# A two-layer graph network in Strassen products: four tasks in the first group, new step orders at the layer change and in layer 1, and a last transition matrix made transposed

## Chip, cores and metric

The kernel runs on one core of a Trainium2 chip. The metric is the device time of that core in microseconds, the median of three runs.

## The reference

128 graphs of 128 nodes with 512 features go through two layers; `x` is 128x128x512 and `adj` 128x128x128.

```python
# layer 0
deg = jnp.sum(adj, axis=-1, keepdims=True)
agg = jnp.einsum('bij,bjf->bif', adj, x) / jnp.maximum(deg, EPS)
out = jnp.einsum('bnf,of->bno', jnp.concatenate([x, agg], axis=2), W)
x = _layernorm(x + jax.nn.relu(out), axis=-1)
# layer 1
e = jax.nn.leaky_relu(sj[:, None, :] + si[:, :, None] + ab[0], negative_slope=0.2)
alpha_matrix = A * jnp.exp(e)
transition = alpha_matrix / (jnp.sum(alpha_matrix, axis=-1, keepdims=True) + 1e-12)
for k in range(Wk.shape[0]):
    H = H + Xk @ Wk[k] + bk[k]
    Xk = jnp.einsum('bij,bjd->bid', transition, Xk)
x = _layernorm(x + jax.nn.relu(H), axis=-1)
```

`sj` and `si` are two linear functions of a node's features, through `Wv` and `aw`; the kernel folds them into two more columns of the big product.

## The kernel before

**Groups and tasks.** The graphs go in 32 groups of four through layer 0, then through layer 1. The products with the weights use a two-level scheme with seven products in the place of eight at each level. An outer product is a *task*, its seven inner products are *steps* (written O5.3: task O5, step 3; inner products in the order 1, 5, 6, 2, 7, 3, 4). A step of layer 0 is two records of 256 columns, one of layer 1 two of 385 (all matmuls come from `mm`, line 149). The left operands of the products are node blocks, transposed on DVE (`x_turn`, L254), and their sums: `x_inner` (L242 to L245) for the inner level, `x_s1` to `x_s4` (L265 to L277) for the outer level, all on POOL. The weights' sums are `w_inner` (L931 to L934) and `w_outer` (L939).

**Lanes.** Tasks run in two lanes of four PSUM banks each, `bA` for lane 0 and `bB` for lane 1. In a task, ACT copies the bank of step 1 (L617) and that of step 2 (L623, into `s`), DVE adds step 3 (L626), the banks of steps 4 and 6 are evicted, the bank of step 5 is read by DVE (L650, L663) and by POOL (L660), that of step 7 late. So a step often has to wait for what ACT or DVE makes of an earlier step of its lane.

**Layer 0.** Group 0 runs one task F, an ordinary 2x2 product of blocks (14 steps of four matmuls), and FL, the product with the adjacency matrices. The other groups run P12, P56, P74 and T (their evictions at L309 to L321 and L355 to L357; `last`, L388, and `residual`, L371). `fold_constants` (L160 to L184) makes the folded columns and the biases; `degree`, `a_norm`, `a_load` and `a_turn` prepare the adjacency matrices.

**Layer 1.** A group runs O1, O2, O5, O6, O7, O4, O3 and C, the two products with the transition matrix. C and O3.7 lag one group and are then written in lower case (c.5, o3.7); x.1 to x.8 is the last C. `sum_r` (L696) and `sum_c` (L704) prepare the sums that C reads. The scores are taken out in `t_scores` (L712 to L723), turned into the transition matrix by `t_load`, `t_exp` (L743, L745), `t_sums` (L750 to L755) and `t_norm` (L762, L770), and transposed in `t_turn` (L777); in the last group `t_exp` and `t_norm` do it in place, with four PE transposes. Layer norm is `ln_mean`, `ln_var` (L493, squares on ACT), `ln_scales` and `ln_apply` (L506, on ACT); `y_store` and `load_y` (L95) keep and fetch the rows, and `load_left` fetches the node blocks.

**Order.** The order of the steps is written out by hand in strings: PA for a group of layer 0, PT for the layer change, PB for a group of layer 1, PL for the last. All else is put beside the steps by tables of positions: PLACES_A, PLACES_B, PLACES_M (last but one group), PLACES_L, PLACES_T (weight loads) and START. Position 2t comes after the instructions of step t, 2t + 1 after its late evictions. `need` checks that what an operation reads was issued before. Each engine's queue, SP's (which issues nearly all DMAs) and POOL's among them, is then taken in the order in which the code is written.

Of the kernel before, what the change touches and what calls it, by code (L numbers as in the profile page):

```python
# [1016 lines left out]
```

## Time and profile before

| | |
|---|---|
| median of three runs | 2112.71 us (2112.41 to 2116.83) |
| time of the profiled execution | 2111.64 us |
| its span | 2109.8 us, so 1.84 us lie outside it |
| granted clock of TensorE, mean | 0.997 |
| instructions | 25967 |
| busy: PE, DVE, ACT, POOL | 2083.5, 1464.6, 1145.5, 1539.4 us |
| PE busy from 0 to 60 us (start) | 53.22 us |
| 60 to 805 (layer 0) | 745.00 us |
| 805 to 864 (layer change) | 54.14 us |
| 864 to 2060 (layer 1) | 1193.61 us |
| 2060 to 2110 (end) | 37.48 us |

The last five rows are the busy time of PE in stretches of the span. PE counts as busy while a matmul is under way or held up inside a row of the timeline, so a short stall between two matmuls does not always show as idle time. In a row of the timeline the first number is the start, the second the length, then come the engine, the line, the destination and sources, the shape and the number of records; in brackets stand the idle time ahead of it and what ended that.

### The profile page before, as it was taken

To read this page: it belongs to the slowest core of one execution; us is meant where nothing else is said; L and a number is where in the kernel's file an instruction comes from. 1 tells how busy PE (TensorE), PEld (TensorE's weight loads), DVE (VectorE), ACT (ScalarE), POOL (GpSimd) and SP (SyncE) were. 2 spreads that over 40 slices of the span, in tenths; PEclk is the share of its full clock that TensorE was granted. 3 is DMA by queue.
4 is the path that set the end of the run, shared out by engine and by line. 5 is a ranking of instruction groups with operands and counts; after the bars stand their busy time and mean duration, and the time that the engine had idled before them with its cause. 6 is when DMAs were issued, how large, how long until landed. Compare 5 with 4: busy or idle time off the path is not lost.

```text
span 2109.8 us, 25967 instructions
## 1 busy us (share of the span) xinstructions
PE 2083.5 (99%) x7104; PEld 1328.1 (63%) x7104; DVE 1464.6 (69%) x3235; ACT 1145.5 (54%) x2879; POOL 1539.4 (73%) x1432
## 2 busy tenths in 40 slices
PE   8999999999999999999999999999999999999997
PEld 5887888888778886555555555555555555555553
DVE  4778777777777776666666666666666666666665
ACT  2665666666656665355455455455455455455454
POOL 5877888887767776767767767767767767767763
PEclk9999999999999999999999999999999999999999
DMA  7766666566566768334434434434434434434423
GB/s 177 183 186 190 189 184 173 159 190 192 160 173 182 191 164 239 76 91 121 109 91 119 112 91 121 109 91 120 111 91 120 111 91 120 111 91 121 110 71 115
DMA packets 429486, 287.13 MB, mean 136 GB/s; under 512 B 153497, under 2 KB 352281, under 8 KB 429340
## 3 DMA queue, kind: packets, MB, share of 16 engines
q1 hardware_dynamic: 428092, 283.62, 50.7%
q10 hardware_dynamic: 1120, 1.84, 0.4%
q8 instruction: 56, 0.92, 0.2%
q14 instruction: 90, 0.74, 0.1%
q0 software_dynamic: 128, 0.01, 0.0%
HBM read 191.60 MB, written 93.79 MB: 135 GB/s over the span
## 4 chain that ended last, share of the span: by engine, by line
PE 95%; DVE 2%; POOL 1%; DMA 1%; ACT 1%; issue 0%; ACTq 0%; SPq 0%; POOLq 0%; DVEq 0%
PE bB L149 50%; PE bA L149 45%; DVE y L371 1%; DVE r L663 1%; DMA xb<-in_x_dram 0%; DMA big<-wd 0%; DMA big<-in_w0t_dram 0%; PE bB L174 0%; POOL s L660 0%; ACT junk L493 0%; POOL r L696 0%; ACT T L762 0%; POOL xs L265 0%; POOL xs L269 0%; POOL xu L277 0%
## 5 line engine op out<-in xcount | busy, mean ns | idle before, releaser
L149 PE MATMUL bA<-big,xu 128*128 128x256 f32 (+1 forms) x1834 | 578.6, 435 | 3.3 <-DVE r L663 1.0
L149 PEld LDWEIGHTS bA<-big,xu 128*128 128x128 f32 x1834 | 345.6, 190 | 177.6 <-issue 25.7
L149 PE MATMUL bB<-big,xl 128*128 128x256 f32 (+1 forms) x1330 | 399.1, 416 | 0.2 <-ACT bB L617 0.2
L149 PE MATMUL bA<-big,xs 128*128 128x256 f32 (+1 forms) x1316 | 387.9, 418 | 0.2
L149 PEld LDWEIGHTS bB<-big,xl 128*128 128x128 f32 x1330 | 252.0, 190 | 99.3 <-issue 15.5
L149 PEld LDWEIGHTS bA<-big,xs 128*128 128x128 f32 x1316 | 245.1, 190 | 92.1 <-DVE bA L626 14.3
L149 PE MATMUL bB<-big,xu 128*128 128x256 f32 (+1 forms) x868 | 286.1, 440 | 2.6 <-DVE bB L388 2.5
L149 PE MATMUL bB<-c,TT 128*128 128x512 f32 x512 | 246.3, 594 | 0.0
L660 POOL TENSOR_TENSOR s<-s,r 128x385 f32<-128x385 f32 x128 | 127.6, 997 | 151.2 <-DVE bA L626 105.3
L493 ACT ACTIVATE junk<-y,mv 128x512 bf16<-128x512 f32 x252 | 181.6, 721 | 78.6 <-POOL mv L488 74.5
L149 PEld LDWEIGHTS bB<-big,xu 128*128 128x128 f32 x868 | 159.0, 189 | 91.7 <-DVE r L650 19.3
L506 ACT ACTIVATE y<-y,mv,rstd 128x512 f32<-128x512 f32 x252 | 201.4, 811 | 1.3 <-POOL mv L501 1.3
L626 DVE TENSOR_TENSOR bA<-bA,s 128x385 f32<-128x385 f32 x128 | 72.5, 567 | 165.6 <-ACT s L623 117.8
L149 PE MATMUL bA<-big,xl 128*128 128x385 f32 (+1 forms) x490 | 181.3, 476 | 4.2 <-DVE xl L254 4.1
L371 DVE SCALAR_TENSOR_TENSOR y<-bB,y 128x512 f32<-128x512 f32 x256 | 170.4, 682 | 19.8 <-PE bB L149 13.5
L149 PE MATMUL bB<-big,xs 128*128 128x385 f32 x448 | 173.5, 492 | 0.9 <-POOL xl L242 0.9
L149 PEld LDWEIGHTS bB<-c,TT 128*128 128x128 f32 x512 | 97.2, 190 | 89.4 <-issue 48.6
L797 ACT COPY bB<-r 128x512 f32<-128x512 f32 x64 | 37.7, 589 | 193.4 <-DVE big L796 188.2
L277 POOL TENSOR_TENSOR xu<-xu,xs 128x896 f32<-128x896 f32 x63 | 131.3, 2085 | 10.3 <-PE bA L149 10.3
L149 PEld LDWEIGHTS bA<-big,xl 128*128 128x128 f32 x490 | 93.3, 191 | 71.0 <-DVE c L663 7.9
L273 POOL TENSOR_TENSOR xl<-xu,xl 128x896 f32<-128x896 f32 x63 | 133.3, 2116 | 1.1
L269 POOL TENSOR_TENSOR xs<-xs,xu 128x896 f32<-128x896 f32 x63 | 131.7, 2090 | 2.4
(172 smaller groups left out, 3540.3 us busy)
## 6 DMA issues: line engine op xcount, KB each, us to landing
xb<-in_x_dram SPq DMA_DIRECT2D x256, 128.0 KB, 3.5
y<-in_x_dram SPq DMA_DIRECT2D x64, 512.0 KB, 4.5
yd<-y SPq DMA_DIRECT2D x64, 512.0 KB, 2.8
xb<-yd SPq DMA_DIRECT2D x256, 128.0 KB, 3.9
y<-yd SPq DMA_DIRECT2D x64, 512.0 KB, 4.4
out_dram<-y SPq DMA_DIRECT2D x62, 512.0 KB, 2.8
ag<-in_adj_dram SPq DMA_DIRECT2D x64, 256.0 KB, 4.0
sb<-sd SPq DMA_DIRECT2D x252, 64.0 KB, 3.1
```

The costliest lines, as they stand in the source:

```text
L149: nc.tensor.matmul(dst, lhsT, rhs, start=start, stop=True, skip_group_check=True)
L269: S_.tensor_sub(xs[n][:, 1], xs[n][:, 0], xu[n][:, 0])
L273: S_.tensor_sub(xl[n][:, 0], xu[n][:, 0], xl[n][:, 0])
L277: S_.tensor_sub(xu[n][:, 1], xu[n][:, 1], xs[n][:, 1])
L371: V.scalar_tensor_tensor(y, t, 0.0, y, ALU.max, ALU.add, accum_out=mvs[n][:, b, 0:1])
L493: L_.activation(junk, ys[n, b // 2][:, b % 2], AF.Square, bias=mvs[n][:, b, 0:1], accum_out=mvs[n][:, b, 1:2])
L506: L_.activation(y, y, AF.Identity, bias=mvs[n][:, b, 0:1], scale=rstds[n][:, b : b + 1])
L626: V.tensor_add(W, X, s5)
L660: S_.tensor_add(s5, s5, part(src, BZ, BW))
L663: V.tensor_add(part(dst, BZ, BW), X, s5)
L797: L_.copy(at_[b], row(b, 254, 766, 1))
```

## The change

**First group.** F becomes four tasks A to D of seven steps with two matmuls each: A and B are the first column of the weight blocks for the upper and lower node blocks, C and D the second. Each uses halves of the banks; C and D are evicted into banks of `bA`. The order is PF. The lanes are swapped (lane 0 now holds `bB`, lane 1 `bA`), and FL runs in `bA`. The inner sums of group 0 move from POOL to DVE, those of the lower blocks into START. Weight slots 1 and 3 are loaded by ACT and SP in turn instead of by ACT alone, `wvt` later on SP. The folding moves from beside F to beside group 1, into `bA`.

**Layer change and layer 1.** New strings PT, PB and PL, a string of its own (PG) for the first group of layer 1, and new positions throughout; PLACES_S gives the work around the layer change its own positions.

**Last group.** Its adjacency matrices come as blocks in four DMAs and are transposed on DVE (`adj_turn`). The matrix of scores is made transposed on PE (`end_scores`, ones times a diagonal of `si`, then Prelu with `sj` as bias, and Exp), multiplied by the transposed adjacency, and its sums over the partitions come from a matmul by ones, which gives them to all partitions (`end_rows`). `end_norm` adds the epsilon, takes the reciprocal and multiplies, in halves of two graphs, on DVE.

```diff
         g = n % NG
+        if n == 2 * NG - 1:
+            adjs[n] = p1.tile([P, G, Q, R], FP, name="agb", tag="ag")
+            load_blocks(adjs[n], adj[g * G : (g + 1) * G])
+            return
...
-    wvt_sb = [p2.tile([P, 2, F], FP, name=f"wvt{i}", tag="y") for i in range(2)]
+    wvt_sb = [p2.tile([P, 2, F], FP, name=f"wvt{i}", tag="c22") for i in range(2)]
...
-    load_w0([nc.scalar], 1)
-    load_w0([nc.scalar], 3)
+    load_w0([nc.scalar, nc.sync], 1)
+    load_w0([nc.scalar, nc.sync], 3)
...
+    def load_wvt():
+        for i in range(2):
+            nc.sync.dma_start(wvt_sb[i], wvt[i * FH : (i + 1) * FH, :].rearrange("(c p) f -> p c f", p=P))
...
-        pb, pc, pw = bB[0], bB[3], bB[0]
+        need(("FL", 0, 2))
+        pb, pc, pw = bA[2], bA[3], bA[2]
         nc.tensor.matmul(pb, ones_row[:K], bk_sb, start=True, stop=True)
...
-        left_sums([S_, S_, S_, S_], [t[:, :, i] for i in range(7)])
+        left_sums([S_ if n else V] * 4, [t[:, :, i] for i in range(7)])
...
+    def first(g, o, h):
+        X, Y, W, Z = [t[:, h * FH : (h + 1) * FH] for t in (bA, bB)[o]]
+        if o == 0:
+            dst = blocks(p2, "c21" if h else "c11")
+            (c21s if h else c11s)[g] = dst
+        else:
+            need(("w_inner", 1))
+
+        def prod(dst, k, start=False):
+            for i in range(2):
+                mm(dst, (xu, xl)[h][g][:, i, LEFT[k]], wf[:, SLOT[2 * i + o], RIGHT[k]], start and i == h == 0)
+
+        def evict(b, t):
+            if o == 0:
+                to = part(dst, b)
+            else:
+                need(("FA", 0, 7), ("FB", 0, 7))
+                to = bA[2 * h + b[0]][:, b[1] * FH : (b[1] + 1) * FH]
+            if (b[0] + b[1]) % 2:
+                L_.copy(to, t)
+            else:
+                V.tensor_copy(to, t)
+        s5 = halves()[:, :FH]
+        if h:
+            need(("F" + "AC"[o], 0, 2))
+        prod(X, 1, True)
+        L_.copy(Y, X)
+        yield
+        prod(Z, 5, True)
+        L_.copy(s5, Z)
+        yield
+        prod(X, 6)
+        V.tensor_add(W, X, s5)
+        yield
+        prod(Y, 2)
+        late.append((evict, BY, Y))
+        yield
+        prod(X, 7)
+        V.tensor_add(Z, X, s5)
+        yield
+        prod(W, 3)
+        late.append((evict, BWW, W))
+        yield
+        prod(X, 4)
+        late.append((evict, BZ, Z))
+        late.append((evict, BX, X))
+        yield
...
-                V.tensor_scalar(dg[:, b], ident, sj[:, b : b + 1], None, ALU.mult)
+                V.tensor_scalar(dg[:, b], ident, si[:, b : b + 1], None, ALU.mult)
...
+    def adj_turn():
+        need(("load_adj", 2 * NG - 1))
+        src = adjs[2 * NG - 1]
+        adjs[2 * NG - 1] = p1.tile([P, G, N], FP, name="agT", tag="aT")
+        V.transpose(adjs[2 * NG - 1].rearrange("p g n -> p (g n)"), src.rearrange("p g j r -> p (g j r)"))
+
+    def end_scores(g):
+        need(("t_scores", g), ("C", g - 1, 8))
+        (dg, _), pt = Ts[g], lanes[0][0]
+        mm(pt, ones[:].to_broadcast([P, P]), dg, True)
+        T = TTs[g] = p1.tile([P, G, N], FP, name="TT")
+        for b in range(G):
+            L_.activation(T[:, b], pt[:, b * N : (b + 1) * N], AF.Prelu, bias=sj[:, b : b + 1], alpha=SLOPE)
+            if b % 2:
+                L_.activation(T[:, b - 1 : b + 1], T[:, b - 1 : b + 1], AF.Exp)
+
+    def end_rows(g, h):
+        need(("end_scores", g), ("adj_turn",))
+        T = TTs[g][:, 2 * h : 2 * h + 2].rearrange("p b n -> p (b n)")
+        pt = lanes[0][1 + h][:, :FH]
+        V.tensor_mul(T, T, adjs[2 * NG - 1][:, 2 * h : 2 * h + 2].rearrange("p b n -> p (b n)"))
+        mm(pt, ones[:].to_broadcast([P, P]), T, True)
+
+    def end_norm(g, h):
+        need(("end_rows", g, h))
+        T = TTs[g][:, 2 * h : 2 * h + 2].rearrange("p b n -> p (b n)")
+        pt = lanes[0][1 + h][:, :FH]
+        rr = halves()[:, :FH]
+        V.tensor_scalar(rr, pt, ROW_EPS, None, ALU.add)
+        V.reciprocal(rr, rr)
+        V.tensor_mul(T, T, rr)
+
...
-        if g == NG - 1:
-            dg, T = T, p1.tile([P, G, N], FP, name="T", tag="aT")
-            pt = lanes[0][0]
-            mm(pt, ones[:].to_broadcast([P, P]), dg, True)
...
-        TTs[g] = p1.tile([P, G, N], FP, name="TT")
-        for b in range(G):
-            pt = lanes[0][1 + b // 2]
-            mm(pt[:, b % 2 * N : (b % 2 + 1) * N], T[:, b], ident, b % 2 == 0)
-            L_.copy(TTs[g][:, b], pt[:, b % 2 * N : (b % 2 + 1) * N])
...
-    lanes = [list(bA), list(bB)]
+    lanes = [[bB[1], bB[3], bB[0], bB[2]], list(bA)]
+    firsts = {c: first(0, *divmod(i, 2)) for i, c in enumerate("ABCD")}
+    TASKS.update({"F" + c: lambda lane, g, c=c: firsts[c] for c in "ABCD"})
...
+    PF = "A.1 A.2 A.3 A.4 A.5 A.6 B.1 B.2 B.3 C.1 B.4 A.7 C.2 B.5 C.3 B.6 B.7 C.4 C.5 C.6 D.1 D.2 D.3 D.4 D.5 D.6 C.7 D.7".split()
-    PT = "p74.5 O1.1 O1.2 p74.6 O1.3 O1.4 p74.7 t.1 t.2 O1.5 O1.6 O1.7 O2.1 t.3 O2.2 t.4 t.5 O2.3 t.6 t.7 t.8 t.9 t.10 t.11 O2.4 O2.5 O2.6".split()
-    PB = ("o3.7 O1.1 O1.2 O2.1 O1.3 O2.2 O1.4 O1.5 O1.6 O1.7 O2.3 O2.4 O5.1 O5.2 O2.5 O5.3 O5.4 O2.6 O5.5 "
-          "O2.7 O6.1 O5.6 O6.2 O5.7 O7.1 O6.3 O7.2 O6.4 O6.5 O7.3 O6.6 O6.7 O7.4 O4.1 O7.5 O4.2 O7.6 O4.3 "
-          "O7.7 O4.4 O4.5 O4.6 c.1 O4.7 O3.1 c.2 O3.2 O3.3 O3.4 c.3 c.4 c.5 c.6 c.7 c.8 O3.5 O3.6").split()
-    PL = ("o3.7 O1.1 O1.2 O2.1 O1.3 O2.2 O1.4 O1.5 O1.6 O1.7 O2.3 O2.4 O5.1 O2.5 O2.6 O5.2 O2.7 O5.3 O5.4 O6.1 O5.5 O5.6 "
-          "O6.2 O5.7 O6.3 O7.1 O6.4 O6.5 O7.2 O7.3 O7.4 O6.6 O7.5 O6.7 O7.6 O7.7 O3.1 O3.2 O3.3 O3.4 c.1 c.2 c.3 c.4 "
-          "O3.5 c.5 c.6 c.7 c.8 O4.1 O3.6 O4.2 O3.7 O4.3 O4.4 O4.5 O4.6 O4.7 x.1 x.2 x.3 x.4 x.5 x.6 x.7 x.8").split()
+    PT = "p74.5 p74.6 O1.1 O1.2 O1.3 p74.7 O1.4 t.1 O1.5 O1.6 t.2 O1.7 O2.1 t.3 O2.2 t.4 t.5 O2.3 t.6 t.7 t.8 t.9 t.10 t.11 O2.4 O2.5 O2.6".split()
+    PG = ("O5.1 O5.2 O5.3 O5.4 O2.5 O2.6 O6.1 O6.2 O5.5 O5.6 O5.7 O7.1 O6.3 O6.4 O7.2 "
+          "O6.5 O2.7 O7.3 O6.6 O7.4 O6.7 O4.1 O4.2 O7.5 O4.3 O7.6 O7.7 O4.4 c.1 O4.5 "
+          "O4.6 c.2 c.3 c.4 O4.7 O3.1 O3.2 O3.3 O3.4 c.5 c.6 c.7 c.8 O3.5 O3.6").split()
+    PB = ("O1.1 o3.7 O1.2 O1.3 O2.1 O2.2 O1.4 O1.5 O1.6 O1.7 O2.3 O2.4 O5.1 O5.2 O5.3 O2.5 O2.6 O5.4 O5.5 "
+          "O2.7 O6.1 O5.6 O6.2 O5.7 O7.1 O6.3 O7.2 O6.4 O6.5 O7.3 O6.6 O6.7 O7.4 O4.1 O4.2 O7.5 O4.3 O7.6 "
+          "O4.4 O7.7 O4.5 c.1 c.2 O4.6 O4.7 O3.1 O3.2 c.3 c.4 O3.3 c.5 O3.4 c.6 c.7 c.8 O3.5 O3.6").split()
+    PL = ("O1.1 o3.7 O1.2 O2.1 O1.3 O2.2 O1.4 O1.5 O1.6 O1.7 O2.3 O2.4 O5.1 O2.5 O5.2 O2.6 O2.7 O5.3 O5.4 O6.1 O5.5 O6.2 "
+          "O5.6 O5.7 O6.3 O7.1 O6.4 O6.5 O7.2 O7.3 O6.6 O7.4 O7.5 O6.7 O7.6 O7.7 O3.1 O3.2 O3.3 O3.4 c.1 c.2 c.3 c.4 "
+          "c.5 c.6 c.7 c.8 O4.1 O3.5 O4.2 O3.6 O3.7 O4.3 O4.4 O4.5 O4.6 O4.7 x.1 x.2 x.3 x.4 x.5 x.6 x.7 x.8").split()
-    for k in range(14):
-        step(0, "F", 0, k + 1)
+    for s in PF:
+        step(2 + "ABCD".index(s[0]), "F" + s[0], 0, int(s[2]))
...
-        for s in PB[PB.index("O5.1") if g == 0 else 0 :] if g < NG - 1 else PL:
+        for s in PL if g == NG - 1 else PB if g else PG:
...
+    def place_op(n, pos, name, m, *a):
+        key = name, m - NG, *a
+        if name not in OWN and key in PLACES_S:
+            at(2 * start_b + PLACES_S[key], OPS[name], m, *a)
+        else:
+            place(n, pos, OPS[name], m - NG if name in OWN else m, *a)
...
+    PLACES_S = {
+        ("ln_apply", -2, 3): 4, ("ln_var", -2, 0): -9, ("sum_c22", -2): -40, ("ln_scales", -2): -1, ("ln_mean", -2): -15,
+        ("x_turn", 1, 0, 1): 55, ("x_inner", 0, 0): -12, ("a_norm", -1): -23, ("ln_var", -1, 3): 58, ("degree", -1): -48,
+        ("a_turn", -1): 27, ("x_s3", 0): 19, ("y_store", -1, 1): 95, ("ln_apply", -1, 1): 79, ("x_inner", 0, 1): -29,
...
-        ("y_store", 0, 1): 280, ("ln_var", 0, 2): 229, ("sum_r", 0, 1): 77, ("load_adj", 0): 129, ("ln_apply", 0, 0): 245,
-        ("ln_apply", 0, 3): 257, ("ln_var", 0, 1): 229, ("load_y", 0, 0): 163, ("x_s2", 1): 71, ("ln_var", 0, 3): 233,
-        ("t_load", 0): 125, ("x_turn", 1, 0, 0): 14, ("t_turn", 0): 189, ("sum_r", 0, 0): 85, ("x_turn", 1, 0, 1): 33,
-        ("y_store", 0, 0): 258, ("load_y", 0, 1): 183, ("ln_apply", 0, 2): 270, ("ln_var", 0, 0): 231, ("t_back", 0): 158,
-        ("t_exp", 0): 140, ("x_s4", 0): 43, ("ln_mean", 0): 224, ("sum_c", 0, 1): 106, ("ln_scales", 0): 233,
-        ("sum_c", 0, 0): 114, ("t_sums", 0): 150, ("x_s3", 1): 84, ("x_s1", 1): 69, ("load_left", 2, 0): 66,
-        ("x_turn", 1, 1, 0): 2, ("t_scores", 0): 116, ("t_norm", 0): 151, ("x_inner", 1, 0): 38, ("x_inner", 1, 1): 25,
-        ("load_left", 2, 1): 38, ("x_turn", 1, 1, 1): 12, ("ln_apply", 0, 1): 256,
+        ("y_store", 0, 1): 281, ("sum_r", 0, 0): 80, ("sum_r", 0, 1): 84, ("sum_c", 0, 0): 115, ("ln_var", 0, 1): 229,
+        ("x_inner", 1, 1): 34, ("load_y", 0, 0): 172, ("ln_var", 0, 3): 233, ("x_turn", 1, 0, 1): 29, ("t_turn", 0): 188,
+        ("t_back", 0): 163, ("ln_var", 0, 2): 225, ("ln_mean", 0): 224, ("ln_apply", 0, 0): 245, ("x_s1", 1): 64,
+        ("load_left", 2, 0): 83, ("y_store", 0, 0): 262, ("ln_apply", 0, 2): 274, ("load_left", 2, 1): 59,
+        ("t_load", 0): 118, ("ln_var", 0, 0): 230, ("ln_apply", 0, 3): 255, ("x_turn", 1, 0, 0): 12, ("ln_scales", 0): 244,
+        ("t_scores", 0): 117, ("t_norm", 0): 151, ("t_exp", 0): 139, ("load_y", 0, 1): 173, ("ln_apply", 0, 1): 255,
+        ("x_s2", 1): 68, ("x_s4", 0): 49, ("x_turn", 1, 1, 0): 1, ("sum_c", 0, 1): 100, ("t_sums", 0): 150, ("x_s3", 1): 96,
+        ("load_adj", 0): 116, ("x_inner", 1, 0): 36, ("x_turn", 1, 1, 1): 16,
...
-        ("end_store", 2): 150, ("t_norm",): 115, ("sum_r", 0): 71, ("end_store", 0): 153, ("t_scores",): 105,
-        ("sum_r", 1): 71, ("t_exp",): 107, ("end_apply", 0): 147, ("load_adj",): 96, ("end_apply", 1): 152,
-        ("load_y", 1): 94, ("end_store", 1): 163, ("t_sums",): 111, ("end_stats", 3): 137, ("end_mean", 0): 125,
-        ("end_apply", 2): 139, ("end_var", 1): 131, ("end_mean", 1): 130, ("end_stats", 2): 130, ("end_rstd", 2): 132,
-        ("load_y", 0): 57, ("end_store", 3): 155, ("end_apply", 3): 151, ("end_scales",): 133, ("end_var", 0): 125,
-        ("sum_c", 0): 76, ("end_rstd", 3): 145, ("sum_c", 1): 76,
+        ("end_store", 2): 158, ("sum_c", 1): 72, ("sum_r", 0): 71, ("end_store", 0): 158, ("t_scores",): 105,
+        ("end_var", 1): 134, ("sum_r", 1): 71, ("load_adj",): 96, ("load_y", 0): 47, ("end_apply", 1): 160,
+        ("load_y", 1): 106, ("end_mean", 1): 128, ("end_rows", 0): 111, ("end_mean", 0): 127, ("end_rstd", 2): 132,
+        ("end_store", 1): 160, ("end_apply", 2): 137, ("end_stats", 2): 129, ("end_store", 3): 162, ("end_scales",): 140,
+        ("sum_c", 0): 76, ("end_rstd", 3): 149, ("end_apply", 0): 144, ("end_scores",): 106, ("end_rows", 1): 111,
+        ("end_norm", 0): 111, ("end_stats", 3): 138, ("end_norm", 1): 111, ("end_apply", 3): 158, ("adj_turn",): 96,
+        ("end_var", 0): 131,
...
-        ("w_inner", 1): 9, ("x_s2", 1): 30, ("fold", 2): 3, ("a_turn", 0): 16, ("w_outer", 2): 16, ("fold", 4): 11,
-        ("degree", 0): 10, ("a_norm", 0): 10, ("load_left", 1, 1): 9, ("x_s1", 1): 21, ("fold", 5): 16, ("fold", 3): 8,
-        ("w_outer", 1): 11, ("fold", 7): 10, ("fold", 6): 17, ("x_s3", 1): 22, ("w_outer", 4): 19, ("load_y", 0, 0): 17,
-        ("load_y", 0, 1): 9, ("x_turn", 1, 0, 0): 14, ("a_load", 0): 15, ("x_turn", 1, 0, 1): 14, ("x_inner", 1, 0): 16,
-        ("x_turn", 1, 1, 1): 18, ("load_left", 1, 0): 12, ("x_turn", 1, 1, 0): 10, ("fold", 1): 4, ("x_inner", 1, 1): 19,
-        ("w_outer", 3): 33, ("load_left", 2, 1): 19, ("load_adj", 1): 26, ("load_left", 2, 0): 23, ("load_wk",): 58,
+        ("fold", 2): 81, ("x_inner", 0, 1): 13, ("load_y", 0, 0): 7, ("fold", 5): 86, ("fold", 4): 85, ("degree", 0): 23,
+        ("load_left", 2, 1): 59, ("x_s3", 1): 50, ("w_outer", 3): 64, ("load_left", 2, 0): 36, ("x_turn", 1, 1, 0): 37,
+        ("x_turn", 1, 0, 1): 39, ("load_left", 1, 1): 17, ("load_y", 0, 1): 13, ("w_inner", 1): 16, ("load_wk",): 74,
+        ("fold", 3): 81, ("x_s2", 1): 54, ("a_norm", 0): 25, ("x_turn", 1, 0, 0): 30, ("fold", 6): 91, ("x_s1", 1): 48,
+        ("w_outer", 1): 22, ("w_outer", 2): 34, ("w_outer", 4): 37, ("load_wvt",): 32, ("fold", 7): 102,
+        ("x_inner", 1, 0): 44, ("a_load", 0): 35, ("x_turn", 0, 1, 1): 8, ("a_turn", 0): 59, ("x_turn", 1, 1, 1): 37,
+        ("load_left", 1, 0): 4, ("fold", 1): 77, ("x_inner", 1, 1): 38, ("load_adj", 1): 47, ("x_turn", 0, 1, 0): 6,
...
-    for p in range(2):
-        run([(x_turn, 0, p, 0), (x_turn, 0, p, 1)])
-    run([(x_inner, 0, 0), (x_inner, 0, 1), (w_inner, 0)])
+    run([(x_turn, 0, 0, 0), (x_turn, 0, 0, 1), (x_inner, 0, 0), (w_inner, 0)])
```

## The prediction

> **What bounds the kernel now.** The page first: TensorE is busy 2083.5 of 2109.8 us, and the chain that ended last is 95% PE.
>
> ```profile
> PE 2083.5 (99%) x7104; PEld 1328.1 (63%) x7104; DVE 1464.6 (69%) x3235; ACT 1145.5 (54%) x2879; POOL 1539.4 (73%) x1432
> PE 95%; DVE 2%; POOL 1%; DMA 1%; ACT 1%; issue 0%; ACTq 0%; SPq 0%; POOLq 0%; DVEq 0%
> ```
>
> Matmul work stays but for a few at the end, so only time in which PE's records don't follow each other can be won. In the chain, in order of time, one landmark recurs every 24.74 us in layer 0 and every 39.55 us in layer 1:
>
> ```profile
> 280.69 6.03 PE bB L149 x20
> 305.44 6.03 PE bB L149 x20
> ...
> 1089.57 5.24 PE bB L149 x12
> 1129.12 5.24 PE bB L149 x12
> ```
>
> Then PE's timeline. A matmul is two records; undisturbed they start 0.216 us (256 columns), 0.3235 (385) or 0.4327 (512) apart. What a row's start-to-next-start has beyond that is lost, even where no idle time is printed. A layer-1 group has 98 records of 385 and 16 of 512: 31.70 + 6.92 = 38.62, so about 0.91 of 39.53 is lost; a layer-0 group loses 0.09.
>
> ```profile
> 1131.53 2.81 PE L149 MATMUL bB<-big,TT 128*128 128x512 f32 x6
> 1134.18 2.45 PE L149 MATMUL bA<-big,xu 128*128 128x385 f32 x6
> 1136.46 1.46 PE L149 MATMUL bB<-big,xu 128*128 128x385 f32 x4
> ...
> 1139.69 3.02 PE L149 MATMUL bB<-big,xu 128*128 128x385 f32 x8
> 1142.55 1.46 PE L149 MATMUL bA<-big,xu 128*128 128x385 f32 x4
> 1143.92 1.53 PE L149 MATMUL bB<-big,xs 128*128 128x385 f32 x4
> 1145.29 0.81 PE L149 MATMUL bA<-big,xu 128*128 128x385 f32 x2
> ...
> 1153.70 1.59 PE L149 MATMUL bA<-big,xs 128*128 128x385 f32 x4
> 1155.13 0.81 PE L149 MATMUL bB<-big,xl 128*128 128x385 f32 x2
> ```
>
> O3.5, O3.6, o3.7: 2.28 - 6 x 0.3235 = 0.34. O1.4 to O1.7: 2.86 - 2.59 = 0.27. Before and in O5.1: 0.08 + 0.08. O6.4, O6.5: 0.14. c.6 to c.8: 0.06.
>
> Last the seams, with their releasers:
>
> ```profile
> 16.41 2.08 PE L149 MATMUL bA<-big,xl 128*128 128x256 f32 x4 [4.13 <-DVE xl L254]
> 819.64 0.70 PE L149 MATMUL bB<-big,xu 128*128 128x256 f32 x2 [2.48 <-DVE bB L388]
> 833.10 1.53 PE L149 MATMUL bB<-big,xs 128*128 128x385 f32 x4 [0.90 <-POOL xl L242]
> 859.01 0.91 PE L149 MATMUL bA<-big,xu 128*128 128x385 f32 x2 [1.01 <-DVE r L663]
> 2083.99 1.12 PE L149 MATMUL bA<-dg,ones 128*128 128x512 f32 x2 [0.79 <-DVE dg L717]
> 2090.26 0.49 PE L149 MATMUL bA<-ident,T 128*128 128x128 f32 x2 [2.22 <-ACT T L762]
> ```
>
> Summed the same way: 7.9 us are lost from 11 to 60, 7.6 from 805 to 864, 7.4 from 2060 to 2101.
>
> **What the Trainium skill says.** "TensorE: Matmul & The Clock Gate", "What's actually happening": after an idle window of about 3.4 us the PE clock is halved. The trace agrees: after the 4.1 us wait the granted clock from 16 to 20 us is 0.57, and eight 128x256 records take 0.43 us each, 1.85 us extra. "VectorE: DVE Perf Modes", "First, the fixed hardware budget": reciprocal iterates, with a repeat count of 8. The trace has it on 128x4 alone (178 ns, against 160 for the reduce L588). "Trainium Architecture — The Big Picture", "Inside one NeuronCore": engines run their own streams and meet only at semaphores; so a late instruction holds those behind it on its engine, as L506 does below.
>
> **First group** (lanes A to D, 28 steps of 0.865). Old: F starts 11.25, stalls 4.29 for xl, loses 1.85 to the slow clock, and F.14 ends about 49.9 with the folding (8 us of PE with its gaps) inside. New: A needs only xu and two weight slots, both there at 11.25. DVE then does x_inner (4 x 0.42, moved from POOL) and w_inner (4 x 0.68) by about 14.1. ACT issues 10 weight DMAs instead of 14 (15.17 / 14 = 1.08 each), so its table load ends about 12.9 and A.1's copy 13.3; A loses about 0.35. xl landed at 15.6, is turned by about 17, and B.2 finds its sum at 17.6 as it wants it (17.7). Slots 1 and 3, now split over ACT and SP, landed by 22 behind 1.25 MB of adj and wvt; without those, before C.1 at 19.4. The steps end at 35.8. Then POOL sets the start of group 1: w_outer 2 x 3.97 from about 25, x_inner of xl 2.9, of xu 2.9: P12.3 waits about 0.8, P56.1 about 0. Folding, moved to bA beside P12 and P56, costs its 8 us there. 35.8 + 0.8 + 8 = 44.6 against 49.9: **-5.2** (-2.6 if POOL or the slots come 2.6 later; -6.5 if nothing waits). wvt and load_wk move behind adj, y and x blocks on SP; wvt lands about 33 and is used past 46. FL.1 wants a_turn at 40; its chain (degree 21 to 23, a_norm to 27.4, store and load 3 each) gives 36.
>
> **Layer change.** The 2.48 us are P74's evictions queued on ACT behind L506 (0.8 each); t.1, which DVE serves after them, now has one more step ahead of it and t.2 two, and ln_apply comes later. x_inner for layer 1 moves 29 and 12 half steps ahead of the seam, so 0.90 goes. In place come neighbours at one step's distance: O1.1 to O1.3, O5.1 to O5.3 and O3.1 to O3.3 (0.23 each, the price of ACT's copy as at 2069.30, where eight records take 2.82), O5.5 to O5.7 and O4.5 to O4.7 (0.27 each), O3.5 0.33, O5.1 0.15. o3.7 has one step more against POOL's two sum_r, x_s3 and L660: 0.6 left. With 0.9 unseen: 3.2 of 7.6, **-4.4** (-2 to -5.5).
>
> **Layer 1, 30 groups.** A step that needs what DVE or ACT makes of a step of its own lane loses 0.23 to 0.34 if only one other step lies between, nothing if two do: so each order is read by its distances. O1.1 now stands between O3.6 and o3.7: -0.34. c.5 has O3.4 behind it: -0.06. O6.2's copy goes ahead of L506 on ACT: -0.14. New: O5.1, O5.2, O5.3 in a row: +0.23. O1.7 and O5.1 stay. O1.5 is close: counted from O3.5's start, ACT now runs O1.1's copy at 2.14, two squares, the four score copies (0.58) and only then O1.2's copy, at 4.63 to 5.09; DVE's add ends 5.69 and O1.5 is due 5.82, so 0 to 0.1: +0.07. Sum **-0.24**, times 30 **-7.2** (-2 to -9). load_y of the second half now follows its y_store on SP and waits for it to land (2.8), with load_left behind; those blocks are turned some 12 us later, so it costs nothing until then. x_s3 goes behind the second sum_r on POOL; O3.5 still comes about 2 us after L660. POOL's x_inner, sums and t_sums keep their order.
>
> **End.** Removed: ACT's four row scalings, four PE transposes (0.86) and four copies, the POOL product, a reduce. Added: two products on DVE (0.43), two matmuls by ones (0.43 each), per half an addition (0.35), a reciprocal, a product (0.4); adj in four DMAs of 64 KB and a 0.70 transpose. Those DMAs go ahead of the second load_y on SP (one of the three y loads ahead of adj in the old order, adj issued 2072.5); landing takes 4.0, DVE reaches the transpose near 2079, and were adj later, every eviction of O3 and O4 behind it on DVE would wait: I cost it at its 0.70, beside PE's own work. After O3.7 ends (2083): dg 2083.9, matmul 2085, Prelu and Exp of half 0 by 2086.2, its product behind O4.5's add, 2087.4; sums 2088.1. On PE, O4.6 and O4.7 (1.3) are queued behind the sums and cover most of what follows. The reciprocal of 128x256 isn't in the trace: nearest row 0.42; eight cycles an element (page above) is 2.3, an estimate. 178 ns for 4 elements fits about five cycles: I take 1.5. Then x.1 starts 2090.4 instead of 2093.29, but DVE does half 1 (2.3) and two evictions before x.1's additions, so x.4 starts about 2095.0 instead of 2096.68: **-1.7** (-4.0 at 0.42; 0 at 2.3). The 9 us tail after PE stays.
>
> **Sum.** -5.2 - 4.4 - 7.2 - 1.7 = -18.5: 2111.64 (span 2109.8 plus 1.8) becomes 2093.1. The median, 2112.71, lies 1.07 above the profiled run: 2094.2.
>
> **Rivals.** (a) New waits in layer 1 pay back all of -7.2: 2101.4. For it: three neighbours stand at one step's distance; against: their price is measured. (b) The seams give half (-2.6, -2.2, 0 at the end): 2100.7. For it: POOL at the start is counted close. (a) and (b) together: 2107.9. (c) Reciprocal cheap, the rest at its better side: about 2089. (d) Slower: ACT at the top of each layer-1 group. O1.2's copy leaves 0.13 us before O1.5. Were it one 0.84 us square later, O1.5 would stall 0.71 + 0.1, and O2's copies, O1's evictions and O5.1's bias copy behind it as much again, together 1.5 us by 30 groups: 45, so 2139. It decides from 0.76 a group (22.7 / 30, to be 0.2% above before). Against: only three squares can stand ahead in the order. That the new orders aren't made is excluded: each engine's list shows them.
>
> **Chances.** Forecast (2090 to 2098) 0.49, (a) 0.20, (b) 0.12, (c) 0.10, both 0.05, (d) 0.04. The range 2087 to 2104 leaves out both, (d), and tails of (a) and (c), under 0.2. About 0.2% (4.2 us) is what a measurement can tell: faster 0.92, same 0.04, slower 0.04.
>
> **What would show it.** Landmarks 39.31 apart instead of 39.55; no loss at o3.7, 0.23 at O5.3, at most 0.1 at O1.5. PE clock 1.00 from 16 to 20. P12.1 of group 1 near 36. Under 1.2 us of stall at each wait of the layer change. x.1 near 21 us before the span's end. A reciprocal far from 1.5, or a wait over 0.3 at O1.5 or O3.2, would make it wrong.

## The result, and the profile after

The median fell from 2113.29 us (2112.41 to 2116.83, four runs, one more than in the table above) to 2095.28 us (2093.67 to 2096.88, four runs). The ratio is 0.9912, with a 95% interval of 0.9894 to 0.9929. The profiled execution took 2095.55 us with a span of 2093.7, so 16.1 us less span than the one shown of before.

The page after, its totals and its chain by engine:

```profile
PE 2075.9 (99%) x7100; PEld 1330.4 (64%) x7100; DVE 1471.0 (70%) x3254; ACT 1152.0 (55%) x2875; POOL 1530.8 (73%) x1423
PE 96%; DMA 1%; POOL 1%; DVE 1%; issue 0%; ACT 0%; ACTq 0%; DVEq 0%; POOLq 0%
```

TensorE is the bound as before. The chain of waits after, its layer-0 and layer-1 landmarks (start, length, what):

```profile
277.18 6.03 PE bA L155 x20
301.94 6.03 PE bA L155 x20
...
1077.42 2.59 PE bB L155 x8
1116.64 2.59 PE bB L155 x8
```

A group of layer 0 takes 24.76 us, as before but for 0.01. A layer-1 group takes 39.22 instead of 39.55. PE's timeline of one layer-1 group after, from O3.5 to O5.3:

```profile
1125.51 1.46 PE L155 MATMUL bB<-big,xu 128*128 128x385 f32 x4
1126.81 0.81 PE L155 MATMUL bA<-big,xu 128*128 128x385 f32 x2
1127.45 0.81 PE L155 MATMUL bB<-big,xu 128*128 128x385 f32 x2
...
1130.69 3.08 PE L155 MATMUL bA<-big,xu 128*128 128x385 f32 x8
1133.60 1.46 PE L155 MATMUL bB<-big,xu 128*128 128x385 f32 x4
1134.97 2.35 PE L155 MATMUL bA<-big,xs 128*128 128x385 f32 x6
1137.17 1.46 PE L155 MATMUL bB<-big,xu 128*128 128x385 f32 x4
```

O3.5 and O3.6 (the first row), O1.1 and o3.7 follow each other at 0.65 a step: the 0.34 at o3.7 is gone. O1.4 to O1.7 take 2.91, 0.32 over the 2.59 of eight records: 0.05 at O1.5 and the old 0.27. O5.1 to O5.3 take 2.20 for six records of 0.3235, so 0.26 over: by the starts of the single records, 0.07 to 0.08 of it at O5.1 is old and 0.17 at O5.2 and O5.3 is new.

The seams after, with their releasers:

```profile
17.64 2.89 PE L155 MATMUL bA<-big,xl 128*128 128x256 f32 x12
26.86 1.13 PE L155 MATMUL bA<-big,xl 128*128 128x256 f32 x4 [0.28 <-DVE bA L477]
37.06 1.13 PE L155 MATMUL bB<-big,xl 128*128 128x256 f32 x4 [0.45 <-ACT bA L458]
845.97 0.91 PE L155 MATMUL bB<-big,xl 128*128 128x385 f32 x2 [0.31 <-DVE c L676]
852.51 0.92 PE L155 MATMUL bB<-big,xu 128*128 128x385 f32 x2 [0.53 <-DVE r L676]
2070.91 1.13 PE L155 MATMUL bB<-TT,ones 128*128 128x256 f32 x4 [1.05 <-DVE TT L760]
2074.37 1.12 PE L155 MATMUL bA<-c,TT 128*128 128x512 f32 x2 [1.04 <-DVE TT L770]
2077.42 3.39 PE L155 MATMUL bA<-c,TT 128*128 128x512 f32 x4 [1.93 <-DVE c L669]
```

The 4.1 us wait for `xl`, the 2.5 at the layer change and the 0.9 at O5.1 of layer 1 are gone. At the end the waits printed for PE before the last C come to 4.8 (0.79, 1.05, 1.04 and 1.93), where they were 3.9 (0.79, 2.22, 0.54 and 0.35), at other places.

Between the starts of the same steps in the two traces the 16.1 us are placed as follows. The last column is what an undo of that part alone costs in medians (runs below).

| stretch | before | after | change | predicted | by undoing it |
|---|---|---|---|---|---|
| start to P12.1 of group 2 | 69.90 | 66.27 | -3.6 | -5.2 | -2.0 |
| 29 groups of layer 0, to P12.1 of group 31 | 717.61 | 717.98 | +0.4 | 0 | |
| to O5.1 of the second layer-1 group | 79.66 | 76.22 | -3.4 | -4.4 | -3.0 |
| 30 layer-1 groups, to O5.1 of the last | 1186.54 | 1176.68 | -9.9 | -7.2 | -9.8 |
| to the end of the span | 56.1 | 56.6 | +0.5 | -1.7 | 0 |
| sum | | | -16.1 | -18.5 | -14.8 |

The +0.4 of layer 0 is an accident of that execution: from P12.1 of group 3 to that of group 31 it took 693.22, in the traces of the twelve other kernels below 692.84 to 692.91, and 692.87 before. The medians differ by 18.0, 2 us more than the traces, mainly because the profiled execution of before was 1.65 below its median. The last column is rough for two rows: the executions without the new start (2095.58 to 2101.3) and without the new layer change (2095.94 to 2100.86) overlap with those of the changed kernel (2093.67 to 2096.88), so there the traces carry the reading. Why the four undone parts sum to 14.8 and not to 18.0 is not settled; beside the later runs the kernel before had medians of 2112.0 to 2113.04 over nine executions each.

### The profile page after: what moved, and what is told of

It reads as the page before. It is cut to its first block, busy times and chain, and to the rows that moved or that the text cites. A ratio compares the mean times of both kernels' runs of the same rounds, so it can differ in the third digit from the quotient of the medians.

```text
span 2093.7 us, 25889 instructions
## 1 busy us (share of the span) xinstructions
PE 2075.9 (99%) x7100; PEld 1330.4 (64%) x7100; DVE 1471.0 (70%) x3254; ACT 1152.0 (55%) x2875; POOL 1530.8 (73%) x1423
## 4 chain that ended last, share of the span: by engine, by line
PE 96%; DMA 1%; POOL 1%; DVE 1%; issue 0%; ACT 0%; ACTq 0%; DVEq 0%; POOLq 0%
PE bA L155 50%; PE bB L155 45%; DMA big<-in_w0t_dram 1%; DMA yd<-y 0%; DMA xb<-in_x_dram 0%; DMA y<-in_x_dram 0%; PE bA L181 0%; POOL s L673 0%; POOL c L717 0%; POOL r L709 0%; DVE s L769 0%; POOL xs L272 0%; POOL xs L276 0%; POOL xu L284 0%; PE bA L191 0%
## 5 line engine op out<-in xcount | busy, mean ns | idle before, releaser
L155 PE MATMUL bB<-big,xu 128*128 128x385 f32 (+1 forms) x1806 | 561.8, 433 | 0.6 <-DVE r L676 0.5
L155 PEld LDWEIGHTS bB<-big,xu 128*128 128x128 f32 x1806 | 341.9, 190 | 167.1 <-issue 44.4
L155 PE MATMUL bA<-big,xl 128*128 128x256 f32 (+1 forms) x1358 | 405.7, 416 | 0.3 <-DVE bA L477 0.3
L155 PE MATMUL bB<-big,xs 128*128 128x256 f32 (+1 forms) x1316 | 384.1, 416 | 0.0
L155 PEld LDWEIGHTS bB<-big,xs 128*128 128x128 f32 x1316 | 249.1, 190 | 84.7 <-ACT bB L630 6.2
L155 PE MATMUL bA<-big,xu 128*128 128x256 f32 (+1 forms) x896 | 294.5, 440 | 0.4 <-DVE bA L639 0.2
L673 POOL TENSOR_TENSOR s<-s,r 128x385 f32<-128x385 f32 x128 | 128.0, 1000 | 182.0 <-DVE bB L639 139.1
L155 PE MATMUL bA<-c,TT 128*128 128x512 f32 x512 | 242.4, 595 | 3.0 <-DVE c L669 1.9
L155 PEld LDWEIGHTS bA<-big,xu 128*128 128x128 f32 x896 | 161.9, 189 | 95.6 <-DVE r L663 19.3
L519 ACT ACTIVATE y<-y,mv,rstd 128x512 f32<-128x512 f32 x252 | 202.1, 815 | 0.6 <-POOL mv L514 0.6
L155 PE MATMUL bA<-big,xs 128*128 128x385 f32 x448 | 173.7, 499 | 0.0
L155 PE MATMUL bB<-big,xl 128*128 128x385 f32 (+1 forms) x462 | 172.0, 480 | 0.8 <-ACT bA L458 0.4
```

Of the source, the lines that this page charges most:

```text
L155: nc.tensor.matmul(dst, lhsT, rhs, start=start, stop=True, skip_group_check=True)
L519: L_.activation(y, y, AF.Identity, bias=mvs[n][:, b, 0:1], scale=rstds[n][:, b : b + 1])
L673: S_.tensor_add(s5, s5, part(src, BZ, BW))
```

## The experiments

**Each part undone alone.** Four kernels are the changed one with one of its four parts put back. Start: task F, its loads, lanes, folding and START.

```diff
-    for s in PF:
-        step(2 + "ABCD".index(s[0]), "F" + s[0], 0, int(s[2]))
+    for k in range(14):
+        step(0, "F", 0, k + 1)
```

> The changed kernel with the old first group (task F, old loads, folding and START positions), all else new. By the two traces the new start wins 3.6 us at the first step of group 2 (69.90 before, 66.27 after), though the clearing of the PSUM banks ahead of it ran 1.21 us longer in the trace of the changed kernel, at a slow clock for longer. If that was chance, the start is worth 4.8: then this kernel takes 2095.3 + 3.6 to 4.8 = 2098.9 to 2100.1, and its first step of group 2 stands near 69.9 when its clearing ends as early as before. The prediction's term (-5.2) gives 2100.5. A rival: the old start with the new layer 0 positions stalls elsewhere, then over 2101.

Measured: 2097.3 us (2095.58 to 2101.3), 2.0 above the changed kernel, less than any theory said. P12.1 of group 2 stands at 68.64, not at 69.90. PE's timeline of this run shows why:

```profile
12.37 1.03 PE L153 MATMUL bA<-big,xu 128*128 128x256 f32 x4
16.71 1.13 PE L153 MATMUL bA<-big,xl 128*128 128x256 f32 x4 [3.31 <-DVE xl L258]
17.68 1.03 PE L153 MATMUL bA<-big,xu 128*128 128x256 f32 x4
```

The clearing of the banks ended later here, so PE waited 3.3 us instead of 4.1 for the same `xl`, and its clock did not drop (a mean of 1.00 from 16 to 20 us, 0.57 before): four records take 1.03 to 1.13 instead of the 2.08 of the row that the prediction shows at 16.41. In three of the four traces with the old start it was so (waits of 2.7 to 3.3; P12.1 of group 2 at 68.28 to 68.64). The clearing itself, the same eight matmul records from 2.66 on, took 5.1 to 6.8 us over the fourteen traces of this study, with either start: they run at half clock until it rises, at 5.5 to 8.9 us. With the new start P12.1 of group 2 stands at 65.59 to 66.50 in ten traces.

Layer change, first attempt: old PT, old order for the first layer-1 group, and the positions of the ordinary groups.

```diff
-    PLACES_S = {
-        ...
+    PLACES_S = {}
```

> The changed kernel with the old order of the layer change, the old order of the first group of layer 1, and the positions of the normal groups there in place of PLACES_S. By the two traces the layer change (P12.1 of group 31 to O5.1 of layer 1's second group) takes 76.22 instead of 79.66: this kernel should give back 3.4, so 2098.7, with a wait near 2.6 at t.1 again. The prediction's term gives 4.4, 2099.7. The new positions of the normal groups may hold more of it: then the wait at t.1 or at O5.1 is larger than before and the time over 2100.

Measured: 2103.45 us, 8.2 above the changed kernel; that stretch took 86.76. The rival held: new waits of 3.4 at O6.7 and 2.3 at O1.5, each followed by 3.4 us at half clock, come on top of the old one at t.2 (2.48). So this was not the old layer change. The second attempt puts each operation in PLACES_S, and the weight loads, at the very place they had in the kernel before:

```diff
-        ("ln_apply", -2, 1): 15, ("ln_var", -1, 3): 58, ("x_inner", 0, 0): -12, ("x_inner", 0, 1): -29,
+        ("ln_apply", -2, 1): 12, ("ln_var", -1, 3): 51, ("x_inner", 0, 0): -13, ("x_inner", 0, 1): -28,
```

> The changed kernel with the layer change undone wholly: old orders, and the work around it at the very places that it had before. The trace's theory: P12.1 of group 31 to O5.1 of layer 1's second group takes 79.5 to 79.7 again instead of 76.1 to 76.2, and the time is 2095.3 + 3.5 = 2098.8. Then the 10 us that the first attempt cost more than this were those of the normal groups' new positions in the old order. The prediction's size, 4.4, gives 80.5 and 2099.7.

Measured: 2098.28 us (2095.94 to 2100.86), 3.0 above the changed kernel. In its trace the stretch takes 80.91, of which some 1.3 is a slower clock behind the wait at t.2 (mean granted clock 0.67 from 816 to 820; the trace of before had the same wait of 2.48 and no drop). Without it, 79.6. Two kernels below that keep the old order of the layer change agree: 80.69 with such a drop, 79.49 without.

Layer 1: PB, PLACES_B and PLACES_M put back.

```diff
-    PB = ("O1.1 o3.7 O1.2 O1.3 O2.1 O2.2 O1.4 O1.5 O1.6 O1.7 O2.3 O2.4 O5.1 O5.2 O5.3 O2.5 O2.6 O5.4 O5.5 "
+    PB = ("o3.7 O1.1 O1.2 O2.1 O1.3 O2.2 O1.4 O1.5 O1.6 O1.7 O2.3 O2.4 O5.1 O5.2 O2.5 O5.3 O5.4 O2.6 O5.5 "
```

> The changed kernel with the old order and positions of the layer-1 groups (PB, PLACES_B, PLACES_M), all else new. If the landmarks (39.22 after, 39.55 before) come from this order alone, they stand 39.55 apart here and the time is 2095.3 + 30 x 0.33 = 2105.2; the losses at o3.7 (0.34), c.8 (0.07) and O6.5 (0.10) are back and those at O5.2 and O5.3 gone. The prediction's sizes give 39.46 and 2102.5. A rival: part of the gain comes from elsewhere (the swapped lanes, the transfers), then the landmarks stay below 39.5.

Measured: 2105.09 us and groups of 39.55: the whole gain of layer 1 is in this order and its positions.

End: the old last group.

```diff
-        need(("end_norm", g, b // 2) if g == NG - 1 else ("t_turn", g))
...
-    PL = ("O1.1 o3.7 O1.2 O2.1 O1.3 O2.2 O1.4 O1.5 O1.6 O1.7 O2.3 O2.4 O5.1 O2.5 O5.2 O2.6 O2.7 O5.3 O5.4 O6.1 O5.5 O6.2 "
+    PL = ("o3.7 O1.1 O1.2 O2.1 O1.3 O2.2 O1.4 O1.5 O1.6 O1.7 O2.3 O2.4 O5.1 O2.5 O2.6 O5.2 O2.7 O5.3 O5.4 O6.1 O5.5 O5.6 "
```

> The changed kernel with the old last group (order, positions, transition matrix made row by row and transposed on PE). By the traces the new end brought nothing: from O5.1 of the last group to the end of the span 56.55 after, 56.09 before. Then this kernel takes 2094.8, 0.5 less than the changed one. The prediction's term (-1.7) gives 2097.0. What tells them apart best is that stretch of the trace: 56.1 by the first, 58.2 by the second.

Measured: 2095.33 us, the same as the changed kernel, and 56.5 in that stretch. The new end is worth nothing.

**Why the end brings nothing.** DVE's timeline at the end, changed kernel:

```profile
2072.10 1.75 DVE L769 RECIPROCAL s<-s 128x256 f32<-128x256 f32 x1
2073.89 0.42 DVE L770 TENSOR_TENSOR TT<-TT,s 128x256 f32<-128x256 f32 x1
2074.23 0.42 DVE L768 TENSOR_SCALAR s<-bB 128x256 f32<-128x256 f32 x1
2074.68 1.75 DVE L769 RECIPROCAL s<-s 128x256 f32<-128x256 f32 x1
2076.47 0.42 DVE L770 TENSOR_TENSOR TT<-TT,s 128x256 f32<-128x256 f32 x1
2076.82 1.02 DVE L669 TENSOR_TENSOR c<-bA,c 128x385 f32<-128x385 f32 x2
```

The two evictions L669 (O4.6 and O4.7) stand behind the second half, and x.2 needs the bank that the first of them frees (it ends 0.05 before x.2 starts): 2077.42, 3.05 after x.1. So they go ahead of it:

```diff
-        ("end_norm", 1): 111,
+        ("end_norm", 1): 115,
```

> The changed kernel with the second half of the last normalisation placed behind the evictions of O4.6 and O4.7 on DVE (they are ahead of the second reciprocal instead of behind it). If the end brings nothing because those evictions hold x.2 (which starts 3.05 us after x.1 and waits for one of them), x.2 comes 2 us earlier, x.4 about 1.2 earlier, and from O5.1 of the last group to the end it takes 55.5 instead of 56.6 to 56.9: 2094.1. If DVE as a whole is the bound (the order of its work does not matter), the stretch stays at 56.6 or more.

Measured: 2093.13 us (2092.93 to 2093.43), 55.3 for the stretch. PE's timeline of this run: x.1 and x.2 in one row, and x.3 waits for the second half.

```profile
2073.61 1.98 PE L155 MATMUL bA<-c,TT 128*128 128x512 f32 x4 [1.04 <-DVE TT L770]
2077.13 1.12 PE L155 MATMUL bA<-c,TT 128*128 128x512 f32 x2 [1.53 <-DVE TT L770]
```

The order is only half of it. In the changed kernel the clock is at half from 2076.87 to 2080.29 (a mean of 0.59 from 2077 to 2081, 1.00 in the run with the evictions first): x.2 and x.3, the row at 2077.42, take 3.23 to the next row where four records at full clock take 1.73. At full clock x.4 would start 42.1 after O5.1 of the last group, an estimate from these two figures and 0.1 for the restart; measured are 43.50 in the changed kernel, 42.07 with the evictions first and 42.97 before. So, by this count, what the swap saved is the slow clock that came with the longer waits. All seven traces of the new end with the old place of the second half have such a drop between x.1 and x.8, none of the three with the new place. The old end has one as well: in the trace of before 3.4 us at half clock from 2091.50 on cost 0.8 between x.1 and x.2, so without either drop the two ends would have x.4 within 0.1 of each other.

**Which edit made the gain of layer 1.** The largest term, tried alone on the kernel before:

```diff
-    PB = ("o3.7 O1.1 O1.2
+    PB = ("O1.1 o3.7 O1.2
...
-        ("t_scores", 0): 116,
+        ("t_scores", 0): 117,
```

> The kernel before with one edit: in PB and PL the first two steps change places (O1.1 ahead of o3.7, and the scores taken half a step later). If a step loses 0.23 to 0.34 because only one other step lies between it and the one it waits for, this alone takes the 0.34 at O3.6 and o3.7 away: landmarks 39.21 instead of 39.55 and 2112.1 - 31 x 0.34 = 2101.6. If the gain of layer 1 needs the new positions of the other work too, the loss moves on to O1.2 or to the scores, and the time stays above 2107.

Measured: 2128.76 us, ratio 1.0077 (1.0065 to 1.009): slower. The 0.34 at o3.7 is gone, but O1.5 waits 0.88 a group, and a group takes 40.11. ACT's timeline of one group in this run:

```profile
1017.63 0.46 ACT L617 COPY bB<-bB 128x385 f32<-128x385 f32 x1 [3.15 <-PE bB L149]
1018.01 0.72 ACT L493 ACTIVATE junk<-y,mv 128x512 bf16<-128x512 f32 x1
...
1018.85 0.72 ACT L493 ACTIVATE junk<-y,mv 128x512 bf16<-128x512 f32 x1
...
1019.70 0.72 ACT L493 ACTIVATE junk<-y,mv 128x512 bf16<-128x512 f32 x1
...
1020.78 0.29 ACT L713 ACTIVATE si<-c,cc 128x2 f32<-128x2 f32 x1
1020.98 0.46 ACT L623 COPY s<-bB 128x385 f32<-128x385 f32 x1
```

Three squares stand between O1.1's copy (L617) and O1.2's (L623). In the changed kernel one of them comes ahead of O1.1's copy. This one number:

```diff
-        ("ln_var", 0, 2): 229,
+        ("ln_var", 0, 2): 225,
```

> The kernel before with O1.1 ahead of o3.7, as in the run that was slower, and with one more number changed: the third of ACT's four layer-norm squares placed at 225 instead of 229, so that it runs ahead of O1.1's copy. In the slower run three squares (0.84 each) and the scores (0.56) stood between the copies of O1.1 and O1.2 on ACT, and O1.5 waited 0.88. With one square less there, O1.2's copy ends about 0.84 earlier: O1.5 loses 0 to 0.1, the landmarks stand 39.20 to 39.30 apart and the time is 2100 to 2104. If the wait has another cause (DVE's addition held by its transposes), it stays above 0.5 and the time above 2120.

Measured: 2103.73 us and groups of 39.26. One square's place is worth 25 us.

**Better orders.** Two edits aim at the losses that stay in the changed kernel, 0.60 a group.

```diff
-          O5.1 O5.2 O5.3 O2.5 O2.6 O5.4 O5.5
+          O5.1 O5.2 O2.5 O5.3 O5.4 O2.6 O5.5
```

> The changed kernel with the part O5.1 to O5.5 of the layer-1 order as it was before (O2.5 between O5.2 and O5.3, two steps between O5.3 and O5.5). By the distances the 0.17 lost at O5.2 and O5.3 go: landmarks 39.04 to 39.05 instead of 39.21, 2095.3 - 30 x 0.17 = 2090.2. If that order was given up because DVE or POOL is late for O2.5 or O2.6 now, a loss of 0.2 or more stands there and the time is 2095 or more.

Measured: 2093.4 us, groups of 39.16. The 0.17 is gone, but 0.12 is lost at O5.5 in its place: a third of the gain expected.

```diff
-          O1.4 O1.5 O1.6 O1.7 O2.3 O2.4 O5.1 O5.2 O5.3 O2.5 O2.6 O5.4 O5.5 O2.7
+          O1.4 O1.5 O2.3 O1.6 O1.7 O2.4 O2.5 O5.1 O5.2 O2.6 O5.3 O5.4 O2.7 O5.5
```

> The changed kernel with O2.3 moved up between O1.5 and O1.6, so that two steps lie between O1.5 and O1.7, and O2.5 moved ahead of O5.1, O2.6 between O5.2 and O5.3, O2.7 between O5.4 and O5.5. By the distances the 0.27 at O1.6 and O1.7 and the 0.17 at O5.2 and O5.3 go: landmarks near 38.78, 2095.3 - 30 x 0.44 = 2082. A rival: O2.5 and O2.6 come too early for POOL's sums and DVE's additions (O2.3 waits for O1.5's result on POOL), then a new loss of 0.2 to 0.5 at O2.5 pays half or all of it back: 2086 to 2095.

Measured: 2292.99 us, 5.0 lost a group ahead of O5.1, ten times the rival's price, and 1.4 to 3.1 more a group, mainly the half clock that follows each of these waits (mean clock 0.965 over the run). In POOL's timeline of a group the sum for O2.3 (L673) now stands ahead of the layer norm's scales (L512 to L514):

```profile
1039.47 1.00 POOL L673 TENSOR_TENSOR s<-s,r 128x385 f32<-128x385 f32 x1 [5.11 <-DVE bB L639]
1040.56 0.19 POOL L512 TENSOR_SCALAR ve<-mv 128x4 f32<-128x4 f32 x1
1040.84 1.03 POOL L513 TENSOR_TENSOR rstd<-ve,nhalf 128x4 f32<-128x4 f32 x1
1041.95 0.20 POOL L514 TENSOR_TENSOR mv<-mv,rstd 128x4 f32<-128x4 f32 x1
```

ACT waits for the last of these with L519, and behind L519 stand O1.6's and O1.7's evictions, `t_exp` and the bias copy of O5.1 (L628):

```profile
1042.18 0.81 ACT L519 ACTIVATE y<-y,mv,rstd 128x512 f32<-128x512 f32 x1 [3.86 <-POOL mv L514]
...
1045.48 0.47 ACT L628 COPY bA<-beta 128x385 f32<-128x385 f32 x1
```

Scales and `t_exp` were moved, together with the end's second half as above:

```diff
-        ("ln_scales", 0): 244, ("t_exp", 0): 139, ("end_norm", 1): 111,
+        ("ln_scales", 0): 243, ("t_exp", 0): 141, ("end_norm", 1): 115,
```

> The changed kernel with the order of the run that lost 5 us a group at O2.5 (O2.3 ahead of O1.6; O2.5, O2.6 and O2.7 each a place or two ahead), the layer norm's scales one half step earlier (243, ahead of O2.3 on POOL), t_exp at 141 (behind O5.1's bias copy on ACT), and the end's second normalisation behind the last evictions. If that loss was POOL's sum for O2.3 standing ahead of the scales, with ACT's ln_apply and then the bias copy of O5.1 waiting for them, it goes: landmarks 38.8 to 38.95, and 2093.1 - 30 x 0.26 to 0.4 = 2081 to 2085. If the order itself is too tight (O2.3's sum on POOL, or the bias copy behind O1.7's eviction), 0.3 to 0.6 is lost at O2.5 or O5.1 instead and the time is 2093 to 2100.

Measured: 2125.53 us, so outside what either theory said, though the 5.0 was gone and O1.5's 0.04 was all that was lost up to O6.2. There O5.7 waited 1.68, behind the row sums on DVE. The last run moves that chain with the steps:

```diff
-        ("t_exp", 0): 141, ("t_sums", 0): 150, ("t_norm", 0): 151, ("x_inner", 1, 0): 36,
+        ("t_exp", 0): 140, ("t_sums", 0): 152, ("t_norm", 0): 155, ("x_inner", 1, 0): 39,
```

> The run before this lost nothing at O1.6, O5.2 and O5.3 any more, but 1.58 a group at O6.2, where O5.7 waits for DVE's addition of O5.5, which stands on DVE behind the row sums of the transition matrix; those came ahead of O5.5 as O5.5 had moved back by one step, and waited for ACT's exponential. Here each piece of that chain moves with the steps: t_exp at 140 (behind O5.1's bias copy, ahead of ln_apply), t_sums at 152 (behind O5.5's addition), t_norm at 155, the inner sums of the upper blocks at 39 (behind t_sums on POOL). If that queue was the cause, the 1.58 goes and landmarks of 38.65 to 38.8 follow (matmuls alone are 38.62): 2093.1 - 30 x 0.41 to 0.56 = 2076 to 2081. If POOL is late now for O6.3 and O6.5 (its inner sums moved back), 0.2 or more is lost at O6.4 to O6.7 and the time is 2085 or more.

Measured: 2075.69 us (2075.23 to 2076.05), ratio to before 0.9826 (0.9813 to 0.984): about twice the gain of the change (some 2 us of it are the end's second half). PE's timeline over O1.4 to O2.5 of one group: each row starts 0.65 a step behind the last, but for 0.04.

```profile
1010.26 1.50 PE L155 MATMUL bA<-big,xu 128*128 128x385 f32 x4
1011.59 0.81 PE L155 MATMUL bB<-big,xu 128*128 128x385 f32 x2
1012.24 1.46 PE L155 MATMUL bA<-big,xu 128*128 128x385 f32 x4
1013.53 1.46 PE L155 MATMUL bB<-big,xu 128*128 128x385 f32 x4
```

A group takes 38.60; its matmuls alone are 38.62 by the prediction's own count.

## Why the prediction was right, and where its terms were not

The mechanism was right: only time in which PE's records don't follow each other could be won, and it was won where the prediction said, in layer 1 above all. That the median came within 1.1 us is in part luck: terms that were too large (start, layer change, end: -11.3 predicted, -6.6 in the traces) met one that was too small (layer 1: -7.2, -9.9), and the profiled run of before was a fast one.

- **First group, -5.2; -3.6 in the traces, -2.0 by undoing.** The step that failed is the term "loses 1.85 to the slow clock", counted as won though it was read from one execution. (The eight records from 16.41 took 3.40 instead of 1.73, so 1.67 is nearer.) The other three traces of the old start don't have it. The prediction named the section "What's actually happening" of the Trainium skill's page "TensorE: Matmul & The Clock Gate" for the drop itself; the same section says that the window runs free and that the cold stretch varies from run to run. The runs agree: 5.1 to 6.8 us for the same clearing, and a drop after a wait of 4.1 but none after 2.7 to 3.3. They differ from it in one point: no whole window of idle time is needed (last section). Chance also shifts the new start: in the trace after, the clearing ended 1.21 later than before, and in the three kernels where it ended as early as before P12.1 of group 2 stands at 65.65 to 65.70, so about 0.6 of the 1.6 that are missing is this. In those three the first six steps lose 0.55 to 0.65 ("A loses about 0.35"), in the trace after nothing. What was not foreseen is B.7, which waits 0.54 for DVE, and D.7, 0.71 for ACT, each with its restart (a matmul released late takes some 0.1 longer to the next start). "P12.3 waits about 0.8" for POOL was too much: 0.12. Folding cost 8.1 beside group 1, as said. P12.1 of group 1 came at 38.03, not near 36. (A step of layer 0 is two matmuls, four records of 256, which is the 0.865 of the sum; the description of the kernel before gives two records.)
- **Layer change, -4.4; -3.4 and -3.0.** The old waits went as said, but one for another reason. "x_inner for layer 1 moves 29 and 12 half steps ahead of the seam, so 0.90 goes" is wrong: it stood 28 and 13 ahead already, as the undo shows. In ACT's timeline of the kernel before, O5.1's bias copy stands behind a square that waits for the layer norm's mean:

```profile
831.80 0.72 ACT L493 ACTIVATE junk<-y,mv 128x512 bf16<-128x512 f32 x1 [5.98 <-POOL mv L488]
...
832.52 0.47 ACT L615 COPY bB<-beta 128x385 f32<-128x385 f32 x1
```

  O5.1 starts at 833.10, 0.11 after that copy. The squares that stood at 51 and 54 moved to 58 and 55, behind O5.1, and in the trace after the copy runs at 824.67, 1.6 ahead of its step. The releaser printed, POOL's L242, had ended at 832.47, so 0.63 before the step. That the moved squares did it is read from these times; no run moved them alone. Of the new waits O4.7 was taken at 0.27 and is 0.58, o3.7 at 0.6 and is 0.80, and 0.46 at O1.5 lay in what was called unseen.
- **Layer 1, -0.24 a group; -0.33.** Gone: 0.34 at o3.7, 0.07 at c.8, 0.13 at O6.4 and O6.5, each as said. New: 0.17 at O5.2 and O5.3 (taken at 0.23) and 0.05 at O1.5 (0.07). Distances and prices held; that ACT leaves O1.2's copy just in time was counted right, and it is the positions that do it.
- **End, -1.7; +0.5 and 0.** The reciprocal takes 1.75, between the 1.5 taken and the estimate of 2.3 (a product on the same tile 0.42). x.1 is 2.4 earlier against the group's start (2.9 said). The failed step is "DVE does half 1 (2.3) and two evictions before x.1's additions, so x.4 starts about 2095.0", 4.6 after x.1: it is 6.3 in the trace (3.4 before). Half 1 takes 2.6, and not only the additions stand behind it, but x.2 itself, by the bank that the first of those evictions frees; yet this alone was priced nearly right: 4.8 without the slow clock. The sum has no term for that clock, which took 1.5 of the 6.3. The run with the evictions first gives 1.3 to 1.6 of it back. x.1 stands 19.4 ahead of the end of the span, not 21.
- **Rivals.** (d) was not this kernel but is one square away from it: with O1.1 moved and ACT's work left in place, O1.5 waits 0.88 (0.81 said). "As much again" behind it did not come, and the total was 2128.8, not 2139.

What stays open: whether the waits of B.7 and D.7 at the start can go without new ones elsewhere was not tried, why 0.12 is lost at O5.5 in the run with the old O5 order was not settled, and neither was why the undone parts sum to less than the whole.

## What to carry to other kernels

In a kernel bound by one engine, count each loss by the distance in steps between an instruction and the one it needs, and then ask on each helper's queue what stands ahead of the instruction that serves it: the same change of order was worth -9 us or +17 us by the place of one 0.84 us activation. When steps move, move the helpers' work with them, piece by piece along the queue that the trace names. Before a loss is counted as won, see whether it is there in more than one execution: two of the four terms here were shifted by a slow clock that came in some executions and not in others.
